# Two-tile score pipelines: 16 heads in four 32-row parts, four score banks, and pipelines that go by pairs of tiles

## The chip, the cores and the metric

The kernel runs on one core of a Trainium2 chip. The metric is the device time of one execution in microseconds (us), taken as the median of several executions. An execution that is profiled also leaves a trace, from which the busy times, the waits and the clock that TensorE was granted are read.

## The reference

`x` has 2 batches of 1024 tokens of width 256; `ctx` has 64 keys per batch. Four blocks follow one another, each a gated cross attention over the 64 keys and a gated feed-forward part:

```python
x = x + tanh(g_xattn[i]) * xattn_i(layernorm(x), ctx, ctx)
x = x + tanh(g_ffn[i]) * ffn_i(layernorm(x))
```

Two of the four attentions matter here: that of block 1 and that of block 3. Both have 16 heads of 16 channels:

```python
qh, kh, vh = heads(q @ Wq + bq), heads(k @ Wk + bk), heads(v @ Wv + bv)
score = einsum('bhqd,bhkd->bhqk', qh, kh) / sqrt(16)
score = where(kv_mask[:, None, None, :], score, -10000.0)   # block 1: one mask of the 64 keys per batch
score = where(m[:, None, :, :] == 0, -1e9, score)  # block 3: a mask for each token and key
attn = softmax(score, axis=-1)
out = einsum('bhqk,bhkd->bhqd', attn, vh) @ Wo + bo
```

The feed-forward part behind block 1's attention is dense: eight gated experts, all of them applied to every token. That behind block 3's attention routes each token to two of eight experts, which needs a router on the attention's result first.

## The kernel before

The 2048 tokens are 16 tiles of 128 (`NT`), in four groups of four (`TG`, `NG`); a group is 512 tokens wide. TensorE works in float32 here, in which one matmul of the program leaves two records in the trace (and two weight loads).

`class Heads` (L420) holds one such attention; there are two objects, `heads1` and `heads3`. `setup` (L431) makes keys and values: `kblk` is the keys in block-diagonal form, so that one matmul over the channels of several heads gives the separate scores of each head, `vblk` the same for the values. For the key mask of `heads1` it also makes `kbias` (L456), whose rows 0 and 1 hold -9984 and -16 where a key is masked and whose other rows are zero; a matmul with a matrix of ones (`ones_b`) adds both to every token. For `heads3` it makes `dropm` (L465), the mask by token and key, which a matmul with the unit matrix (`ident_b`) adds to the scores.

`pipeline` (L636) runs over the tiles one by one. In each round it calls, for different tiles, the four steps:

- `scores` (L520) takes two banks of PSUM (`ps_s`) for one tile. The mask goes in first by two matmuls of 512 columns (L536). Then four matmuls (L542), each with 64 channels (four heads) as its rows, add the scores: rows 0 to 63 into one bank, rows 64 to 127 into the other, 256 columns each. VectorE takes the maximum of each bank by head (L562) and subtracts it (L563); ScalarE takes the exponential of all 1024 columns (L572). In `heads3` the first bank (`by_head`, L429) goes another way: VectorE takes the negative maximum (L555), and ScalarE makes subtraction and exponential in one, head by head, eight instructions of 64 columns (L558); only the second bank is subtracted on VectorE, and its exponential is L570.
- `turned` (L575) transposes the result on TensorE, eight matmuls of 128 columns (L584) into two banks, which ScalarE copies to `pT` (L181).
- `quotients` (L592) makes, with matmuls of 32 columns of weights (L603), the denominators (`halves`) and the weighted values (`vblk`) of all heads in one bank. ScalarE makes the reciprocal through a logarithm (L615, L616), and VectorE multiplies and refines it (L617 to L619).
- `output` (L627) applies the last weights (L273 with `wo`) and adds the gated result to `xs` (L634).

Beside these, `between` advances two lists of generators: `ready`, which makes the norm, its transposes (L265) and the queries (`query_steps`, L505: L273 with `wq`, L511) of the group ahead, and `onward`, which makes what comes after for the group behind: in `heads1` the norm and the transposed input of the dense feed-forward part, in `heads3` the norm and the router's logits.

The order in which instructions stand on each engine is not that of the calls alone: the program is scheduled when it is built, so parts of one step may stand between parts of another. Buffers come from pools. In `middle` (L1776), which runs `heads1`, PSUM's eight banks are shared out as 4 for scores (`ps`), 2 for transposes (`pt`) and 2 for queries, quotients and outputs (`py`). In `last_attention` (L1866), which runs `heads3`, they are 3, 2 and 2, and 1 for the router (`pr`). The dense part after `heads1` (`ffn1_group`; L1676, L1374 and L1721 are matmuls of it) takes its banks when these pools end.

Of the kernel before, what the change touches and what calls it, by code (L numbers as in the profile page):

```python
# [8 lines left out]
F32 = mybir.dt.float32  # L9
# [35 lines left out]
def kernel(ctx: ExitStack, tc: tile.TileContext, a: dict, out: bass.AP):  # L45
# [372 lines left out]


    class Heads:  # L420


        def __init__(self, pre, c_bk, r_bv, r_bo, gate, key_mask, full_mask):
            self.pre, self.c_bq, self.c_bk, self.gate = pre, c_bk - 1, c_bk, gate
            self.r_bv, self.r_bo = r_bv, r_bo
            self.key_mask, self.full_mask = key_mask, full_mask
            self.live, self.qT = {}, {}

            self.by_head = 0 if full_mask is None else 1  # L429

        def setup(self, psp, tag):  # L431
# [11 lines left out]
            if key_mask is not None:  # L443
# [7 lines left out]
                two_rows = held.tile([P, 2], F32, name="two_rows")  # L451
                V.tensor_scalar(two_rows[:, 0:1], partid, 0.0, 9984.0, ALU.is_equal, ALU.mult)
                V.tensor_scalar(two_rows[:, 1:2], partid, 1.0, 16.0, ALU.is_equal, ALU.mult)
                V.tensor_add(two_rows[:, 0:1], two_rows[:, 0:1], two_rows[:, 1:2])
                self.kbias = held.tile([P, B * SK], BF16, name="kbias")
                V.tensor_scalar(self.kbias, km, -1.0, two_rows[:, 0:1], ALU.add, ALU.mult)  # L456
# [63 lines left out]
        def scores(self, tt, pools):  # L520

            b, t = tt // (NT // B), tt % TG
            two, pss = pools["two"], pools["ps"]
            pr = two.tile([P, H, SK], F32, name="pr")
            prv = pr.rearrange("p (c r j) k -> p r c j k", c=NC, r=2)
            HC = H // NC


            pair = [pss.tile([P, 512], F32, name="ps_s") for _ in range(2)]

            if self.full_mask is not None:
                whose, drop = ident_b, self.dropm[:, tt, :]
            else:
                whose, drop = ones_b, self.kbias[:, b * SK : (b + 1) * SK]
            for r in range(2):
                T.matmul(  # L536
                    pair[r], lhsT=whose, rhs=drop.unsqueeze(1).to_broadcast([P, HC, SK]),
                    start=True, stop=False, skip_group_check=True,
                )
            for c in range(NC):  # L540
                for r in range(2):
                    T.matmul(  # L542
                        pair[r][:, c * 256 : (c + 1) * 256],
                        lhsT=self.qT[tt // TG][r * 64 : (r + 1) * 64, c, t * P : (t + 1) * P],
                        rhs=self.kblk[r * 64 : (r + 1) * 64, b, c, r * 4 : (r + 1) * 4]
                        .rearrange("p j k -> p (j k)"),
                        start=False, stop=True, skip_group_check=True,
                    )
            for r in range(2):
                ps3 = pair[r].rearrange("p (j k) -> p j k", k=SK)  # L550
                ps4 = pair[r].rearrange("p (c j k) -> p c j k", c=NC, k=SK)
                mx = two.tile([P, HC], F32, name="mx")
                if r < self.by_head:

                    V.tensor_reduce(mx, ps3, AX.X, ALU.max, negate=True)  # L555
                    for j in range(HC):
                        c, k = divmod(j, HC // NC)
                        A.activation(  # L558
                            prv[:, r, c, k], ps3[:, j], AF.Exp, bias=mx[:, j : j + 1]
# [4 lines left out]
                    prv[:, r], ps4,  # L564
                    mx.rearrange("p (c j) -> p c j", c=NC).unsqueeze(3)
                    .to_broadcast([P, NC, HC // NC, SK]),
                    ALU.subtract,
                )
                if self.by_head:
                    A.activation(prv[:, r], prv[:, r], AF.Exp)  # L570
            if not self.by_head:
                A.activation(pr, pr, AF.Exp)  # L572
            self.live[tt] = pr

        def turned(self, tt, pools):  # L575
# [4 lines left out]
            for q4 in range(2):  # L580
                pst = pt.tile([P, 512], F32, name="ps_tr")
                for i in range(4):
# [3 lines left out]
                        pr[:, 2 * hp : 2 * hp + 2, :].rearrange("p a k -> p (a k)"),  # L586
# [49 lines left out]
        def pipeline(self, pools, ready, onward):  # L636
# [9 lines left out]
            for i in range(NT + 2):  # L646
                if i < NT and i % TG == 0:
                    advance(coming, 99)
                    if i + TG < NT:
                        coming.append(ready(i // TG + 1))  # L650
                if 0 <= i - 1 < NT:
                    self.turned(i - 1, pools)
                if i < NT:
                    self.scores(i, pools)
                between(2)
                if 0 <= i - 1 < NT:
                    self.quotients(i - 1, pools)
                between(2)
                if 0 <= i - 2:
                    self.output(i - 2, pools)  # L660
                if i > TG and i % TG == 1:
                    gone.append(onward(i // TG - 1))
# [1113 lines left out]
    def middle():  # L1776
        with ExitStack() as es:
# [4 lines left out]
            with ExitStack() as wide:  # L1782
                def wpl(name, bufs, **kw):
# [6 lines left out]
                    "pt": wpl("pt", 2, space=PSUM), "ps": wpl("ps", 4, space=PSUM),  # L1790
                    "py": wpl("py", 2, space=PSUM),
                }
                hp, hTp = wpl("h", 2), wpl("hT", 2)
# [20 lines left out]
            class Both:  # L1814


                @staticmethod
                def tile(shape, dtype, name):
                    return py.tile(shape, dtype, name="ps_y")

# [45 lines left out]
    def last_attention():  # L1866
        with ExitStack() as es:
            def pool(name, bufs, **kw):
# [7 lines left out]
                "two": pool("two", 3), "nq": 2, "by_log": True, "pt": pool("pt", 2, space=PSUM),  # L1876
                "ps": pool("ps", 3, space=PSUM), "py": pool("py", 2, space=PSUM),
# [129 lines left out]
```

## Time and profile before

| What | Value |
|---|---|
| Median of three executions | 2232.72 us (2231.45 to 2238.72) |
| The profiled execution | 2234.43 us |
| Its span | 2232.7 us |
| Mean granted clock of TensorE | 0.947 of full speed |
| TensorE (PE) busy | 2057.9 us, 92% of the span |
| VectorE (DVE) busy | 1333.7 us, 60% |
| ScalarE (ACT) busy | 940.6 us, 42% |
| GpSimd (POOL) busy | 1124.9 us, 50% |
| First and last score matmul (L542) | 348.4 and 2026.0 us |

The span is the time from the first to the last instruction of the profiled execution; 1.7 us of its time lie around it. PE is the matmuls, PEld the loads of weights into TensorE, which go on beside matmuls. A record's length is latency as well as work, so what a matmul occupies is read from the distance between the starts of records. In the rows of the slices each digit is a fortieth of the span, in tenths: 9 is busy for 90% or more, and the clock row shows the clock granted to TensorE. An arrow in brackets names what ended an engine's idle time before an instruction.

### The profile page before, as it was taken

The numbers are of one execution on the slowest core, as the hardware profiler recorded it, in microseconds if no ns is written. First come the engines' busy times: TensorE is split into PE (matmuls) and PEld (weight loads), VectorE is DVE, ScalarE is ACT, GpSimd is POOL, SyncE is SP. The second block draws the span as 40 slices with busy tenths as digits, with TensorE's granted clock in tenths as the row PEclk, the third lists the DMA queues.
The fourth block names the chain that finished last, engine by engine and source line by source line (L and its number), as shares of the span: only waits on it lengthen the run. The fifth ranks groups of instructions, "written<-read, shape, count | busy, mean of one in ns | idle before, by whom it ended". The sixth has DMA issues, their size and how long they took to land. (4 is left out here: it accounts for less than half of the span.)

```text
span 2232.7 us, 31616 instructions
## 1 busy us (share of the span) xinstructions
PE 2057.9 (92%) x11296; PEld 1733.4 (78%) x11296; DVE 1333.7 (60%) x3059; ACT 940.6 (42%) x2124; POOL 1124.9 (50%) x1265
## 2 busy tenths in 40 slices
PE   5659998999999999999999999999986999797897
PEld 3449985688888788888888887888864998465797
DVE  6841127856666666666666567566675566677464
ACT  4424435643333433333433333333332555473454
POOL 3226644136666456666466664666630664210673
PEclk9859998999999999999999999999985999797899
DMA  3146451012222222222222222222231444111352
GB/s 112 39 164 191 101 168 58 6 62 85 88 91 86 76 93 87 85 85 85 82 88 85 85 88 82 85 85 90 90 96 45 130 123 121 52 39 58 103 148 60
DMA packets 108533, 201.05 MB, mean 90 GB/s; under 512 B 20053, under 2 KB 47961, under 8 KB 105791
## 3 DMA queue, kind: packets, MB, share of 16 engines
q1 hardware_dynamic: 83144, 162.18, 22.7%
q0 software_dynamic: 19728, 36.03, 6.3%
q8 instruction: 90, 1.47, 0.3%
q10 hardware_dynamic: 5504, 0.82, 0.2%
q14 instruction: 67, 0.54, 0.1%
HBM read 206.89 MB, written 21.91 MB: 102 GB/s over the span
## 5 line engine op out<-in xcount | busy, mean ns | idle before, releaser
L1676 PE MATMUL ps_b<-xsum,w 128*128 128x256 f32 x1536 | 385.7, 380 | 0.1
L1307 POOL TENSOR_TENSOR w<-w 128x256 f32<-128x256 f32 x220 | 163.1, 742 | 376.3 <-DMA w<-in_L_Wu_dram 191.1
L1676 PEld LDWEIGHTS ps_b<-xsum,w 128*128 128x128 f32 x1536 | 290.7, 190 | 45.6 <-issue 4.5
L1358 ACT COPY u<-ps_b 128x512 f32<-128x512 f32 (+5 forms) x242 | 118.9, 491 | 436.0 <-PE ps_b L1721 252.6
L1676 PE MATMUL ps_a<-hT,w 128*128 128x256 f32 x1024 | 265.0, 380 | 0.2 <-ACT ps_b L1340 0.2
L1676 PEld LDWEIGHTS ps_a<-hT,w 128*128 128x128 f32 x1024 | 193.4, 190 | 27.1 <-ACT ps_b L1340 0.9
L1308 POOL TENSOR_TENSOR w<-w 128x256 f32<-128x256 f32 x220 | 192.2, 874 | 0.0
L1310 POOL TENSOR_TENSOR w<-w 128x256 f32<-128x256 f32 x220 | 183.4, 834 | 16.6
L1309 POOL TENSOR_TENSOR w<-w 128x256 f32<-128x256 f32 x220 | 190.4, 866 | 0.0
L1340 ACT COPY ps_b<-ps_a 128x512 f32<-128x512 f32 (+5 forms) x242 | 115.4, 477 | 120.4 <-DVE b L1706 68.7
L1702 DVE TENSOR_TENSOR c<-ps_e,u 128x512 f32<-128x512 f32 x64 | 44.2, 691 | 153.9 <-ACT u L1358 153.9
L1738 POOL TENSOR_TENSOR m<-m,accT 128x256 f32<-128x256 f32 x60 | 71.7, 1195 | 125.7 <-ACT m L1346 125.7
L1346 ACT COPY m<-ps_e 128x512 f32<-128x512 f32 (+5 forms) x242 | 117.9, 487 | 38.0 <-PE ps_e L1721 26.3
L1676 PE MATMUL ps_e<-hT,w 128*128 128x256 f32 x512 | 133.2, 382 | 0.0
L1676 PE MATMUL ps_e<-xsum,w 128*128 128x256 f32 x512 | 132.9, 380 | 0.0
L1721 PE MATMUL ps_b<-t,w 128*128 128x256 f32 x512 | 131.9, 382 | 0.2 <-DVE accT L1739 0.2
L1721 PE MATMUL ps_a<-b,w 128*128 128x256 f32 x512 | 131.4, 379 | 0.0
L250 POOL TENSOR_SCALAR h<-xs,rstd,off 128x256 f32<-128x256 f32 x32 | 19.9, 632 | 220.3 <-DVE off L242 121.6
L1703 DVE TENSOR_TENSOR b<-b,c 128x512 f32<-128x512 f32 x128 | 117.1, 915 | 4.3
L1683 ACT ACTIVATE b<-b 128x512 f32<-128x512 f32 x128 | 80.7, 630 | 67.1 <-DVE b L1691 62.7
L1676 PEld LDWEIGHTS ps_e<-hT,w 128*128 128x128 f32 x512 | 97.3, 191 | 14.7 <-ACT m L1346 1.2
L1721 PEld LDWEIGHTS ps_b<-t,w 128*128 128x128 f32 x512 | 97.6, 191 | 14.0 <-DVE accT L1739 0.7
(419 smaller groups left out, 4488.8 us busy)
## 6 DMA issues: line engine op xcount, KB each, us to landing
w<-in_L_Wg_dram SPq DMA_DIRECT2D x64, 512.0 KB
w<-in_L_Wu_dram SPq DMA_DIRECT2D x64, 512.0 KB
w<-in_L_Wd_dram SPq DMA_DIRECT2D x64, 512.0 KB
w<-in_L_W_dram SPq DMA_DIRECT2D x64, 512.0 KB
hd_L<-h SPq DMA_DIRECT2D x8, 512.0 KB
b<-b2d SPq DMA_DIRECT2D x23, 128.0 KB
xs<-in_x_dram SPq DMA_DIRECT2D x4, 512.0 KB
xd<-xs SPq DMA_DIRECT2D x4, 512.0 KB
```

The source lines that it names most:

```text
L1307: lambda: eng.tensor_add(s[0], a21, a22),
L1308: lambda: eng.tensor_sub(s[1], s[0], a11),
L1309: lambda: eng.tensor_sub(s[2], a11, a21),
L1310: lambda: eng.tensor_sub(s[3], a12, s[1]),
L1340: A.copy(self.b, self.pa)
L1346: A.copy(self.sb5, self.pe)
L1358: A.copy(u2, self.b)
L1676: T.matmul(ps[:, q * 256 : (q + 1) * 256], lhsT=lhs[kind][:, q, :], rhs=xr[kind], start=(first and q == 0), stop=True, skip_group_check=True,)
L1683: done[0] = A.activation(dst, src, AF.Silu)
L1703: V.tensor_mul(m[name], m[name], c)
L1721: T.matmul(ps, lhsT=wd[kind][:, q, :], rhs=m["rhs"][kind][:, q * 256 : (q + 1) * 256], start=(clear and q == 0), stop=True, skip_group_che ...
L1738: G.tensor_add(sb, sb, acc[:, i, j])
```

## The change

The change has three parts.

1. `scores` takes a pair of tiles instead of one. The 16 heads lie in four parts of 32 channels (two heads each) instead of two of 64. Part r of both tiles goes into bank r of four, with matmuls of 32 rows and 128 columns that are placed on rows 32r to 32r+31 of the array (`tile_position`): 16 matmuls a pair instead of 8. VectorE and ScalarE then work bank by bank, a bank being one part of both tiles: as many reductions, subtractions and exponentials for a pair as before. `pr` has two buffers of a pair each. `by_head` becomes 2 of 4 banks, the same share as 1 of 2.
2. The key mask of `heads1` is one row in each of the four 32-row parts (`kbias` with -100, weights `hundred` with 100), so that a pair takes four matmuls of 32 rows and 512 columns. The mask of `heads3` stays a matmul with the unit matrix over all 128 rows: eight of 256 columns for a pair, where there were four of 512.
3. `pipeline` goes over pairs: `turned` of the first tile, `scores` of the next pair, `quotients` of the first, `turned` of the second, `output` of the tile before, `quotients` of the second, `output` of the first. The pools `pt` and `py` become one: 4 banks for scores and 4 for all else in `middle`, 4 and 3 and the router's 1 in `last_attention`.

In the changed file the lines move. The masks are L554 (`heads1`) and L546 (`heads3`), the scores L566, the maxima L579 (by head) and L585, the exponential by head L581, the subtraction L586, the exponential L594, the transposes L606, the matmuls of `quotients` L625, its logarithm and exponential L637 and L638, its products L639 to L641, the addition to `xs` L656.

```diff
--- before.py
+++ after.py
@@ -416,6 +416,16 @@
                             active[k] = None
                             at[k] += 1
 
+    def one_tag(pool):
+
+
+        class Tagged:
+            @staticmethod
+            def tile(shape, dtype, name):
+                return pool.tile(shape, dtype, name="ps_y")
+
+        return Tagged
+
 
     class Heads:
 
@@ -426,7 +436,7 @@
             self.key_mask, self.full_mask = key_mask, full_mask
             self.live, self.qT = {}, {}
 
-            self.by_head = 0 if full_mask is None else 1
+            self.by_head = 0 if full_mask is None else 2
 
         def setup(self, psp, tag):
 
@@ -448,12 +458,15 @@
                 km = held.tile([P, B * SK], F32, name="km")
                 V.tensor_single_scalar(km, km_u.bitcast(U8), 0.0, ALU.not_equal)
 
-                two_rows = held.tile([P, 2], F32, name="two_rows")
-                V.tensor_scalar(two_rows[:, 0:1], partid, 0.0, 9984.0, ALU.is_equal, ALU.mult)
-                V.tensor_scalar(two_rows[:, 1:2], partid, 1.0, 16.0, ALU.is_equal, ALU.mult)
-                V.tensor_add(two_rows[:, 0:1], two_rows[:, 0:1], two_rows[:, 1:2])
                 self.kbias = held.tile([P, B * SK], BF16, name="kbias")
-                V.tensor_scalar(self.kbias, km, -1.0, two_rows[:, 0:1], ALU.add, ALU.mult)
+                V.memset(self.kbias, 0.0)
+                for r in range(4):
+                    V.tensor_scalar(
+                        self.kbias[32 * r : 32 * r + 1, :], km[32 * r : 32 * r + 1, :],
+                        -1.0, 100.0, ALU.add, ALU.mult,
+                    )
+                self.hundred = held.tile([P, P], BF16, name="hundred")
+                V.memset(self.hundred, 100.0)
             if full_mask is not None:
                 m_w = wpool.tile([P, 2048], F32, name="w")
                 m_i = m_w[:, : NT * SK].rearrange("p (t k) -> p t k", k=SK).bitcast(I32)
@@ -517,60 +530,69 @@
             xg = xs[:, g * TG : (g + 1) * TG, :]
             G.tensor_add(xg, xg, self.bo.unsqueeze(1).to_broadcast([P, TG, D]))
 
-        def scores(self, tt, pools):
-
-            b, t = tt // (NT // B), tt % TG
+        def scores(self, pp, pools):
+
+
+            b = pp // (NT // 2 // B)
             two, pss = pools["two"], pools["ps"]
-            pr = two.tile([P, H, SK], F32, name="pr")
-            prv = pr.rearrange("p (c r j) k -> p r c j k", c=NC, r=2)
-            HC = H // NC
-
-
-            pair = [pss.tile([P, 512], F32, name="ps_s") for _ in range(2)]
+
+            pr = two.tile([P, 2 * NC, 4, 2, SK], F32, name="pr", bufs=2)
+            banks = [pss.tile([P, 512], F32, name="ps_s") for _ in range(4)]
 
             if self.full_mask is not None:
-                whose, drop = ident_b, self.dropm[:, tt, :]
+                for u in range(2):
+                    drop = self.dropm[:, 2 * pp + u, :]
+                    for r in range(4):
+                        T.matmul(
+                            banks[r][:, u * 256 : (u + 1) * 256], lhsT=ident_b,
+                            rhs=drop.unsqueeze(1).to_broadcast([P, 4, SK]),
+                            start=(u == 0), stop=False, skip_group_check=True,
+                        )
             else:
-                whose, drop = ones_b, self.kbias[:, b * SK : (b + 1) * SK]
-            for r in range(2):
-                T.matmul(
-                    pair[r], lhsT=whose, rhs=drop.unsqueeze(1).to_broadcast([P, HC, SK]),
-                    start=True, stop=False, skip_group_check=True,
-                )
-            for c in range(NC):
-                for r in range(2):
+                for r in range(4):
+                    at = slice(32 * r, 32 * r + 32)
                     T.matmul(
-                        pair[r][:, c * 256 : (c + 1) * 256],
-                        lhsT=self.qT[tt // TG][r * 64 : (r + 1) * 64, c, t * P : (t + 1) * P],
-                        rhs=self.kblk[r * 64 : (r + 1) * 64, b, c, r * 4 : (r + 1) * 4]
-                        .rearrange("p j k -> p (j k)"),
-                        start=False, stop=True, skip_group_check=True,
+                        banks[r], lhsT=self.hundred[at, :],
+                        rhs=self.kbias[at, b * SK : (b + 1) * SK].unsqueeze(1)
+                        .to_broadcast([32, 8, SK]),
+                        start=True, stop=False, skip_group_check=True,
+                        tile_position=(32 * r, 0),
                     )
-            for r in range(2):
-                ps3 = pair[r].rearrange("p (j k) -> p j k", k=SK)
-                ps4 = pair[r].rearrange("p (c j k) -> p c j k", c=NC, k=SK)
-                mx = two.tile([P, HC], F32, name="mx")
+            for u in range(2):
+                t = (2 * pp + u) % TG
+                for c in range(NC):
+                    for r in range(4):
+                        at = slice(32 * r, 32 * r + 32)
+                        T.matmul(
+                            banks[r][:, (u * NC + c) * P : (u * NC + c + 1) * P],
+                            lhsT=self.qT[2 * pp // TG][at, c, t * P : (t + 1) * P],
+                            rhs=self.kblk[at, b, c, 2 * r : 2 * r + 2]
+                            .rearrange("p j k -> p (j k)"),
+                            start=False, stop=True, skip_group_check=True,
+                            tile_position=(32 * r, 0),
+                        )
+            for r in range(4):
+                ps3 = banks[r].rearrange("p (j k) -> p j k", k=SK)
+                mx = two.tile([P, 8], F32, name="mx")
                 if r < self.by_head:
 
                     V.tensor_reduce(mx, ps3, AX.X, ALU.max, negate=True)
-                    for j in range(HC):
-                        c, k = divmod(j, HC // NC)
+                    for j in range(8):
                         A.activation(
-                            prv[:, r, c, k], ps3[:, j], AF.Exp, bias=mx[:, j : j + 1]
+                            pr[:, j // 2, r, j % 2], ps3[:, j], AF.Exp, bias=mx[:, j : j + 1]
                         )
                     continue
                 V.tensor_reduce(mx, ps3, AX.X, ALU.max)
                 V.tensor_tensor(
-                    prv[:, r], ps4,
-                    mx.rearrange("p (c j) -> p c j", c=NC).unsqueeze(3)
-                    .to_broadcast([P, NC, HC // NC, SK]),
+                    pr[:, :, r], banks[r].rearrange("p (a j k) -> p a j k", j=2, k=SK),
+                    mx.rearrange("p (a j) -> p a j", j=2).unsqueeze(3)
+                    .to_broadcast([P, 2 * NC, 2, SK]),
                     ALU.subtract,
                 )
-                if self.by_head:
-                    A.activation(prv[:, r], prv[:, r], AF.Exp)
-            if not self.by_head:
-                A.activation(pr, pr, AF.Exp)
-            self.live[tt] = pr
+            for u in range(2):
+                mine = pr[:, u * NC : (u + 1) * NC, self.by_head :]
+                A.activation(mine, mine, AF.Exp)
+            self.live[2 * pp] = self.live[2 * pp + 1] = pr
 
         def turned(self, tt, pools):
 
@@ -583,7 +605,7 @@
                     hp = q4 * 4 + i
                     T.transpose(
                         pst[:, i * P : (i + 1) * P],
-                        pr[:, 2 * hp : 2 * hp + 2, :].rearrange("p a k -> p (a k)"),
+                        pr[:, tt % 2 * NC + hp // 4, hp % 4].rearrange("p a k -> p (a k)"),
                         ident,
                     )
                 evac(1, pT[:, q4 * 4 : q4 * 4 + 4, :].rearrange("p i q -> p (i q)"), pst)
@@ -643,23 +665,34 @@
                 advance(coming)
                 advance(gone, n)
 
-            for i in range(NT + 2):
-                if i < NT and i % TG == 0:
+
+            for i in range(NT // 2 + 2):
+                if i < NT // 2 and 2 * i % TG == 0:
                     advance(coming, 99)
-                    if i + TG < NT:
-                        coming.append(ready(i // TG + 1))
-                if 0 <= i - 1 < NT:
-                    self.turned(i - 1, pools)
-                if i < NT:
+                    if 2 * i + TG < NT:
+                        coming.append(ready(2 * i // TG + 1))
+                a = 2 * (i - 1)
+                valid = 0 <= a < NT
+                if valid:
+                    self.turned(a, pools)
+                if i < NT // 2:
                     self.scores(i, pools)
                 between(2)
-                if 0 <= i - 1 < NT:
-                    self.quotients(i - 1, pools)
+                if valid:
+                    self.quotients(a, pools)
                 between(2)
-                if 0 <= i - 2:
-                    self.output(i - 2, pools)
-                if i > TG and i % TG == 1:
-                    gone.append(onward(i // TG - 1))
+                if valid:
+                    self.turned(a + 1, pools)
+                if 0 <= a - 1:
+                    self.output(a - 1, pools)
+                if a > 0 and a % TG == 0:
+                    gone.append(onward(a // TG - 1))
+                between(2)
+                if valid:
+                    self.quotients(a + 1, pools)
+                between(2)
+                if valid:
+                    self.output(a, pools)
                 between(1)
             advance(gone, 99)
 
@@ -1787,9 +1820,9 @@
 
                 pools = {
                     "two": wpl("two", 3), "nq": 2, "by_log": True,
-                    "pt": wpl("pt", 2, space=PSUM), "ps": wpl("ps", 4, space=PSUM),
-                    "py": wpl("py", 2, space=PSUM),
+                    "ps": wpl("ps", 4, space=PSUM), "py": wpl("py", 4, space=PSUM),
                 }
+                pools["pt"] = one_tag(pools["py"])
                 hp, hTp = wpl("h", 2), wpl("hT", 2)
 
                 def ready(g):
@@ -1811,13 +1844,7 @@
             hTp = es.enter_context(tc.tile_pool(reuse_waits="tile", name="mi_hT", bufs=1))
             py = es.enter_context(tc.tile_pool(reuse_waits="tile", name="mi_py", bufs=2, space=PSUM))
 
-            class Both:
-
-
-                @staticmethod
-                def tile(shape, dtype, name):
-                    return py.tile(shape, dtype, name="ps_y")
-
+            Both = one_tag(py)
             pools = {"two": two, "pt": Both, "ps": Both, "py": py}
 
             def last(g):
@@ -1873,9 +1900,10 @@
             hp, hTp, hp2, rp = pool("h", 2), pool("hT", 2), pool("h2", 2), pool("r", 2)
             pr = pool("pr", 1, space=PSUM)
             pools = {
-                "two": pool("two", 3), "nq": 2, "by_log": True, "pt": pool("pt", 2, space=PSUM),
-                "ps": pool("ps", 3, space=PSUM), "py": pool("py", 2, space=PSUM),
+                "two": pool("two", 3), "nq": 2, "by_log": True,
+                "ps": pool("ps", 4, space=PSUM), "py": pool("py", 3, space=PSUM),
             }
+            pools["pt"] = one_tag(pools["py"])
             with tc.issue_after(done[0].ins):
                 A.preload_act_table_set("natural_log_exp_and_others")
             router3.open()
```

## The prediction

> **What bounds the kernel now.** I read the page's busy rows and slices first, then cut the two stretches in which the changed functions run into windows of 20 us.
>
> ```profile
> PE 2057.9 (92%) x11296; PEld 1733.4 (78%) x11296; DVE 1333.7 (60%) x3059; ACT 940.6 (42%) x2124; POOL 1124.9 (50%) x1265
> PE   5659998999999999999999999999986999797897
> PEclk9859998999999999999999999999985999797899
> ```
>
> TensorE is busy nearly throughout. The changed functions are two stretches: the pipeline of `heads1` (338 to 457 us) and that of `heads3` (1895 to 2045 us).
>
> ```profile
> core 0: us, PE busy (x) PEld busy (x) DVE busy (x) ACT busy (x) POOL busy (x), PEclk, DMA share, GB/s
> 380.00:400.00 20.00, 20.00 (x187) 13.04 (x186) 15.27 (x44) 13.69 (x29) 4.55 (x5) 1.00 0.01 3
> 400.00:420.00 20.00, 19.64 (x183) 12.86 (x182) 14.33 (x37) 13.26 (x26) 1.09 (x2) 1.00 0.05 14
> 420.00:440.00 20.00, 19.54 (x214) 13.10 (x214) 18.19 (x46) 11.07 (x22) 0.00 (x0) 1.00 0.01 2
> ...
> 1960.00:1980.00 20.00, 19.42 (x192) 13.32 (x191) 12.87 (x46) 15.53 (x48) 4.54 (x5) 1.00 0.16 54
> 1980.00:2000.00 20.00, 19.90 (x157) 12.16 (x157) 16.44 (x66) 15.13 (x47) 1.09 (x2) 1.00 0.13 45
> 2000.00:2020.00 20.00, 19.90 (x232) 14.66 (x232) 16.09 (x70) 13.07 (x42) 0.00 (x0) 1.00 0.11 37
> ```
>
> In both, TensorE leaves 0 to 0.6 of 20 us open at full clock, so a microsecond less of its work is worth up to a microsecond. Behind it VectorE has 13 to 18 of 20 us filled and ScalarE 11 to 15.5: the room is a fifth to a third.
>
> The tile view of the scores and the timeline of TensorE give durations and order.
>
> ```profile
> L542 PE MATMUL ps_s<-kblk,qT x256: 376/376/792, 348.5 to 2026.4; 64*128 64x256 f32 x128
> L558 ACT ACTIVATE pr<-ps_s,mx x128: 296/330/407, 1926.1 to 2034.5; 128x64 f32<-128x64 f32 x128
> L562 DVE TENSOR_REDUCE mx<-ps_s x48: 655/681/692, 353.4 to 2027.1; 128x8 f32<-128x512 f32 x48
> ```
>
> ```profile
> 352.11 2.93 PE L542 MATMUL ps_s<-kblk,qT 64*128 64x256 f32 x12 [2.96 <-ACT qT L511]
> ...
> 394.80 0.59 PE L536 MATMUL ps_s<-kbias,ones_b 128*128 128x512 bf16 x2
> 395.32 1.13 PE L542 MATMUL ps_s<-kblk,qT 64*128 64x256 f32 x8
> 396.38 0.65 PE L603 MATMUL ps_y<-pT,halves 128*32 128x128 f32 x16
> 396.85 0.62 PE L603 MATMUL ps_y<-pT,vblk 128*32 128x128 f32 x16
> 397.39 1.13 PE L273 MATMUL ps_y<-wo,oT 128*128 128x256 f32 x4
> ...
> 448.74 1.04 PE L584 MATMUL ps_tr<-ident,pr 128*128 128x128 f32 x8
> 458.76 1.08 PE L265 MATMUL ps_tr<-ident,h 128*128 128x128 f32 x6 [1.32 <-POOL h L250]
> ```
>
> A float32 matmul leaves two records, and a record's length holds its latency, so I take the distance of starts: masks 0.53 us a tile (394.80 to 395.32), scores 1.06, the 32 records of L603 1.01. Within the scores the single records start in twos, 6 to 7 ns apart, each two 0.213 us after the last: 4 x 0.213 = 0.85, which leaves 0.2 us for going into and out of the 64-row tiling. L603's records start in fours, 7 ns apart, one such round each 0.109 us.
>
> **The change, part by part** (counts from the order of TensorE's instructions in the changed program).
>
> *Key masks of `heads1`.* 32 matmuls of 512 columns, 0.265 us each with their share of the wait (8.5 us; 0.216 is the column time), become 8 sets of four 32-row matmuls which, side by side, cost 0.216 + 0.05 each: 2.1 us. I count the column time alone, 6.9 - 2.1 = -4.8 us. In `heads3` 32 of 512 columns become 64 of 256: no saving in columns; at most -1.4 by 0.88 a pair for 1.06. I take 0.
>
> *Scores.* Per pair of tiles 8 x 0.213 = 1.7 us becomes, if four 32-row tiles run abreast, 8 x 0.109 = 0.87. No row shows a 32-row tile. The nearest are L542 (two row tiles abreast) and L603 (four column tiles abreast, 128 columns), and I take L603's 0.109. The Trainium skill speaks a little against it: "TensorE: Matmul & The Clock Gate", Measured speedup, has four row tiles at 3.07 times one, not 4; worked from L603's row that would be an estimated 32 x 0.109 / 3.07 = 1.14 us a pair, so 0.27 x 16 pairs = 4.3 us of the gain lost. The scheduler also cuts the 16 matmuls of a pair into pieces, between which other work stands: `heads1` has 22 pieces and 43 rounds of 0.218 (32 if uncut) for some 25 pieces and 40 rounds of 0.426 before: 9.4 for 17.0 us and three entries of 0.2 less, -8.2. `heads3` has 30 pieces and 48 rounds: 10.5 for about 15.5, with some 8 entries more (+1.6): -3.4. That each entry costs is measured (the 0.2 us above), and the skill's "TensorEngine Tiling (Array Packing)", Key Properties, says the same of changing the mode: the cut pairs of `heads3` are where the tiling pays least.
>
> TensorE's work thus falls by 13.0 us in `heads1` and 3.4 in `heads3`. VectorE and ScalarE keep their work: as many 128x512 reductions, subtractions and exponentials. What changes is when.
>
> *Filling the pipeline.* Before, the first transposes (L584 at 357.2) need one tile's four VectorE passes. Now L606 of tile 0 needs the pair's exponential, which needs eight passes of 0.60 us spacing, 4.8 us, behind all 16 score matmuls. From the queries' end I get 359.4: +2.2. In `heads3` some +1.5.
>
> *One set of score banks.* Four banks hold one pair, so a pair's masks (L554, L546) wait for the subtractions (L586) of the pair before: bank 3 comes free 4.8 us after the scores end. Before, a tile took two of four banks (three in `heads3`). TensorE has about 4.2 us of other work placed there (L606, L625, L273), so about 0.6 us stays, and the next L625 waits for pT copies on ScalarE queued behind the pair's exponentials (2 x 0.62 to 1.06): about 1 us a pair, 8 us, less the 2.5 us of such waits that `heads1` has now: +5.5. Bounds: 0 if other work always fits, and 8 x 2.2 = 18 if the masks find none of the last half of the block covered. Behind a waiting mask in TensorE's order stand the transposes and queries that feed ScalarE.
>
> *`heads3` by head.* The first two of four banks go head by head: 16 exponentials. Eight take 1.76 us in the timeline, so 3.5 us, plus two halves of 0.62: a block of 4.8 us on ScalarE in which pT, the logarithms L637/L638 and qT wait, where now it is 2.4 us (1.76 + 0.67) a tile. PSUM for transposes and outputs shrinks from four banks to three. Extra wait between 0 and 2.4 us a pair; ScalarE is filled to three quarters here, so I take 0.9: 8 x 0.9 = +7.
>
> *End of `heads1`.* The dense part's banks now include those of the joined pool, used until the last norm's transposes; these (L265, eight records) now stand ahead of the first down-projection matmuls. The 1.32 us wait at 458.76 grows to about 3.6 by my placing: +2.3. The trace shows what follows a long pause: after the 2.96 us of waiting before 352.11 the granted clock is half for 3.41 us (0.79 over the window of 340 to 360); after 1.32 us here it stayed full. One such step costs up to half of 3.41: +1.7. The lowest bound of this part is 0.
>
> *Handovers.* Each pair has some four more crossings that nothing hides (L554, L606, L625, L273 after another engine); which my placing took as free; by an estimate of 0.06 us each, half of the smallest wait of 0.15 us that the timeline of VectorE names there, 16 x 4 x 0.06 = +4, from 0 to 8. The waits above hold a part of it, so +2.
>
> *Set-up.* Memsets and one-row operations (L461 to L469) replace as many small ones, 0.2 to 0.4 us each, on VectorE long before the stretch. Nothing; 1 us if that cover were gone. The queues of SP and POOL keep their order.
>
> Sum: `heads1` -13.0 + 2.2 + 5.5 + 2.3 + 1.7 = -1.3; `heads3` -3.4 + 1.5 + 7 = +5.1; handovers +2: +5.8 on 2234.4 (span 2232.7 and 1.7 around it) gives 2240.2. The profiled run is itself 1.7 us above the median of the runs shown, so against the median I get 2238.5 to 2240 and write 2240.
>
> **Rivals.** About 0.3%, 6.7 us, is what a measurement of this kernel can tell from no change.
>
> 1. *Coupling* (0.45): as summed. For it: VectorE's block of 4.8 us and ScalarE's 15.5 of 20 us. 2236 to 2254, nine tenths above +0.3%.
> 2. *Waits and savings cancel* (0.20): the stalls of `heads3` are near 0.3 us a pair rather than 0.9, no clock step: 2234.4 + 5.8 - 4.8 - 1.7 = 2233.
> 3. *TensorE stays the bound, faster* (0.25): the windows that show 20.00 of 20 us speak for it. The saving -16.4 is kept, with fills +3.7 and end +2.3 and a stall of at most 0.2 us a pair (+3.2) less 2.5 of waits that go: -9.7, about 2224, or 2217 without fill and end. It decides where the stalls and handovers of a pair are under 0.5 us.
> 4. *Row tiles do not run abreast* (0.10): 32 x 0.109 = 3.5 us a pair for 2.1 now, 16 x 1.4 = +22, masks of `heads1` saving nothing: about 2256. Two abreast instead of four is a milder form: scores save nothing, 2242 to 2246.
>
> So faster 0.25 (rival 3), within 0.3% 0.25 (rival 2 and a tenth of the first), slower 0.50. The range 2218 to 2257 leaves out the best of rival 3 and the worst of 1 and 4; the likeliest case alone is 2236 to 2254.
>
> **What would show it.** L566 records starting in fours, rounds of 0.109 us; if in ones or twos, rival 4. TensorE's idle time ahead of L554 and L546 released by L586, ahead of L625 by L181; if the sum in 360 to 440 us is under 4 us, rival 3. The end of `heads1`: an idle stretch over 3 us before L265 and a clock under 1.00 just after. In `heads3`: L581 in blocks of 3.5 us and idle TensorE behind them. The start of the dense part and the end of `heads3`, set against before, give the share of each. It is wrong if the dense part starts over 5 us earlier.

## The result, and the profile after

The changed kernel takes 2260.8 us (median of four, 2251.77 to 2267.5) against 2234.26 us before (median of four too): 1.0102 times as long, interval 1.0075 to 1.0129, so some 23 us slower (17 to 29). The profiled execution took 2255.67 us, 21 us more than that of before. The sign was forecast; the size was 6 us, and 2260.8 lies outside the range of 2218 to 2257.

The page of the changed kernel, the same rows as before: TensorE has almost the same busy time, for less work, as will be seen; a fortieth of the span is too coarse a slice to show where.

```profile
PE 2055.9 (91%) x11584; PEld 1747.2 (78%) x11584; DVE 1334.8 (59%) x3061; ACT 941.0 (42%) x2124; POOL 1121.7 (50%) x1265
PE   6659998899999999999999999999986999796797
PEclk9869998999999999999999999999985999897899
```

The windows of the two stretches tell more (the columns are as before; the clock is the third number from the right).

```profile
380.00:400.00 20.00, 17.84 (x150) 12.47 (x150) 12.42 (x38) 11.72 (x25) 2.16 (x4) 0.83 0.01 3
400.00:420.00 20.00, 17.20 (x199) 12.16 (x198) 17.48 (x37) 9.98 (x19) 2.63 (x1) 0.91 0.00 1
420.00:440.00 20.00, 17.69 (x210) 13.26 (x208) 15.79 (x43) 12.69 (x24) 1.09 (x2) 0.95 0.06 15
440.00:460.00 20.00, 16.19 (x198) 12.26 (x196) 12.45 (x35) 11.18 (x23) 1.09 (x2) 0.88 0.00 1
...
1980.00:2000.00 20.00, 17.36 (x179) 13.88 (x180) 10.96 (x38) 13.18 (x41) 3.19 (x5) 0.83 0.15 54
```

Where TensorE left 0 to 0.5 us open at a clock of 1.00, it now leaves 2 to 4 open, and its clock is 0.83 to 0.95. The timeline of TensorE shows one such place:

```profile
376.74 0.66 PE L265 MATMUL ps_y<-ident,h 128*128 128x128 f32 x4
377.33 0.39 PE L554 MATMUL ps_s<-kbias,hundred 32*128 32x512 bf16 x2
378.55 0.37 PE L554 MATMUL ps_s<-kbias,hundred 32*128 32x512 bf16 x1 [0.83 <-DVE pr L586]
379.15 0.37 PE L554 MATMUL ps_s<-kbias,hundred 32*128 32x512 bf16 x1 [0.23 <-DVE pr L586]
379.15 0.71 PE L566 MATMUL ps_s<-kblk,qT 32*128 32x128 f32 x12
380.87 2.07 PE L273 MATMUL ps_y<-wo,oT 128*128 128x256 f32 x4 [1.00 <-DVE oT L641]
382.74 1.06 PE L265 MATMUL ps_y<-ident,h 128*128 128x128 f32 x4
383.59 1.91 PE L606 MATMUL ps_y<-ident,pr 128*128 128x128 f32 x8
```

The masks of the next pair wait for the last banks of the pair before; once the scores are in, the output's matmul waits for L641, whose turn on VectorE comes behind the block of score passes. Then the clock goes to half from 380.1 to 386.9 us: the four matmuls of `wo` at 380.87 last 2.07 us where they took 1.13 before, the eight transposes 1.91 where they took 1.09.

The waits of TensorE from 340 to 480 us, the longest rows:

```profile
PE ps_y L265 <- POOL h L250: 7.3, 4, 3.5
PE ps_s L554 <- DVE pr L586: 4.4, 7, 1.4
PE ps_y L273 <- DVE oT L641: 3.9, 4, 1.0
```

The counterparts of the first two before, from 340 to 460 us (L536 is the mask, L563 the subtraction; no wait for L641's counterpart, L619, is in its list):

```profile
PE ps_tr L265 <- POOL h L250: 2.5, 3, 1.3
PE ps_s L536 <- DVE pr L563: 0.3, 1, 0.3
```

To sum a stretch up I take it from the first query matmul of `heads1` to the 120th matmul of the dense part, and split it into time without a matmul or weight load (idle), the loss by half clock (half of the busy time that lies in half-clock stretches), and the rest, TensorE's work at full clock. This work is the length of records and so holds latency.

| | to last score | from there | total | idle | loss by half clock | work |
|---|---|---|---|---|---|---|
| before | 99.8 | 44.4 | 144.2 | 7.5 | 2.2 | 134.4 |
| change | 99.2 | 61.2 | 160.5 | 21.1 | 16.2 | 123.2 |

The work did fall, by 11.2 us. Idle time rose by 13.6, and half clock took another 14.0: +16.3. For `heads3`, from its first score to the 20th matmul of the experts behind it, the same split (work, half clock, idle; rounded) gives 160.0 us = 116.8 + 16.6 + 26.5 before and 167.4 = 111.0 + 18.6 + 37.7 with the change: less work by 5.8, 11.2 more idle, 1.9 more by the clock: +7.4. Each profile is one execution: where the code of a stretch is the same, it repeated within 2 us in `heads1` and within 5 in `heads3` in the profiles below.

### The profile page after: what moved, and what is told of

Read it like the earlier page. It is cut to its first block, busy times and chain, and to the rows that moved or that the text cites. A ratio compares the mean times of both kernels' runs of the same rounds, so it can differ in the third digit from the quotient of the medians.

```text
span 2253.6 us, 32177 instructions
## 1 busy us (share of the span) xinstructions
PE 2055.9 (91%) x11584; PEld 1747.2 (78%) x11584; DVE 1334.8 (59%) x3061; ACT 941.0 (42%) x2124; POOL 1121.7 (50%) x1265
## 5 line engine op out<-in xcount | busy, mean ns | idle before, releaser
L1343 POOL TENSOR_TENSOR w<-w 128x256 f32<-128x256 f32 x220 | 183.2, 833 | 16.6
L250 POOL TENSOR_SCALAR h<-xs,rstd,off 128x256 f32<-128x256 f32 x32 | 18.2, 579 | 230.7 <-DVE off L242 138.1
L1709 PEld LDWEIGHTS ps_e<-hT,w 128*128 128x128 f32 x512 | 97.2, 191 | 15.9 <-ACT m L1379 2.9
L1709 PEld LDWEIGHTS ps_e<-xsum,w 128*128 128x128 f32 x512 | 97.1, 191 | 15.2 <-issue 1.8
```

Of the source, the lines that this page charges most:

```text
L1343: lambda: eng.tensor_sub(s[3], a12, s[1]),
L1709: T.matmul(ps[:, q * 256 : (q + 1) * 256], lhsT=lhs[kind][:, q, :], rhs=xr[kind], start=(first and q == 0), stop=True, skip_group_check=True,)
```

## The experiments

Three theories stood. W: the pairing makes TensorE wait, and what is taken from TensorE is only waited away. R or T: the row tiling itself is dear. B: TensorE bounds, as the windows of before suggest. All ratios are to the kernel before on the same chip.

**e1, the key mask alone**, in the kernel before:

```diff
-whose, drop = ones_b, self.kbias[:, b * SK : (b + 1) * SK]
+at, n = slice(64 * r, 64 * r + 64), 64
+whose, drop = self.hundred, self.kbias[:, b * SK : (b + 1) * SK]
...
-    pair[r], lhsT=whose, rhs=drop.unsqueeze(1).to_broadcast([P, HC, SK]),
+    pair[r], lhsT=whose[at, :],
+    rhs=drop[at].unsqueeze(1).to_broadcast([n, HC, SK]),
```

> The kernel before, with one thing of the change alone: the key mask of heads1 by one row in each of two 64-row parts, two matmuls side by side for a tile instead of two one after the other. Tiles stay single, pools stay. Theory W (the loss is waits of TensorE that the pairing of tiles makes, and half-clock steps that follow them): nothing here makes a wait, TensorE bounds the stretch, so 16 x 0.216 = 3.5 us less work, and up to 16 x 0.1 more where mask and scores share a tiling mode: 2.5 to 5 us faster than before. Theory R (32- and 64-row tiling costs more than it saves): no gain, 0 to 3 us slower.

1.0002 (0.999 to 1.0014): no gain, or 2 us at most. In the profile the work of the first stretch fell from 134.4 to 130.0 us, idle rose from 7.5 to 10.5, and the stretch took 143.2 us for 144.2. Two rows of its waits show where it went; the first stood at 1.0 us, three times, before:

```profile
PE ps_tr L589 <- ACT pr L577: 3.3, 4, 1.0
PE ps_y L273 <- DVE oT L624: 1.5, 1, 1.5
```

Transposes now wait for the exponentials. The kernel before was thus hardly bound by TensorE alone: a stretch whose windows show 98 to 100% busy had almost nothing to give for 4.4 us less work. That speaks against B, and it is what the prediction's first step got wrong.

**e2 and e3, the change in one stretch only** (the other class and its pools as before).

> The whole change in heads1 only; heads3 and its pools as before. The profiles put the end of the dense part 13.4 us later with the change, the rest of the 21 us behind it. Theory W: the two stretches are independent, so +12 to +15 us. Theory H (heads3, where sixteen exponentials by head stand in a row on ScalarE and the banks are one fewer, carries the loss, and the first stretch's delay is made up in the rest): +2 to +6 us.

> The whole change in heads3 only; heads1 and its pools as before. Theory W: what e2 leaves, +5 to +9 us. Theory H: +15 us or more.

1.0071 (1.0051 to 1.0092), some 16 us, and 1.0053 (1.0033 to 1.0073), some 12 us. Both lose; which loses more the intervals (11 to 21 us and 7 to 16) do not tell. Their sum, 1.0124, agrees with the change within the intervals. H's 2 to 6 us for e2 falls; W's 5 to 9 us for `heads3` lies at the low end of e3's interval.

**e4, pairs without 32-row tiling**: each bank holds one half of the heads of one tile, and the masks are those of before.

```diff
+pair = banks[2 * u : 2 * u + 2]
...
-    banks[r][:, (u * NC + c) * P : (u * NC + c + 1) * P],
-    lhsT=self.qT[2 * pp // TG][at, c, t * P : (t + 1) * P],
+    pair[r][:, c * 256 : (c + 1) * 256],
+    lhsT=self.qT[tt // TG][r * 64 : (r + 1) * 64, c, t * P : (t + 1) * P],
```

> The change without its tiling: pairs of tiles, four banks, joined pools and the order by pairs stay, but the scores are the 64-row matmuls of 256 columns of before, each bank holding one half of the heads of one tile, and the masks are the full-row ones of before. TensorE has about 13 us more work in heads1 than in the changed kernel, and a bank pair is complete after half of the matmuls. Theory W (the pairing makes the waits): as slow as the change or slower, +15 to +30 us over before, with half-clock steps in both stretches. Theory R (the tiling is what costs): the pairing alone is near before, -3 to +6 us.

1.0036 (1.0023 to 1.005), some 8 us: between the two theories. Its `heads3` takes 159.6 us, as before (160.0), with the pools of the change there; the half that goes head by head is one bank of each tile, so that eight exponentials stand together and not sixteen. It has 8.4 us more work in the first stretch than the change and is still 9.0 us shorter there (151.5), with a loss by half clock of 4.5 instead of 16.2 us.

**e5, the tiling undone but the banks kept**: 64-row matmuls into banks that still hold one part of both tiles.

```diff
-for r in range(4):
-    at = slice(32 * r, 32 * r + 32)
+for r in (0, 2, 1, 3):
+    at = slice(64 * (r // 2), 64 * (r // 2) + 64)
...
-        tile_position=(32 * r, 0),
```

> The changed kernel with its four banks, each holding one part of the heads of both tiles, its masks, its pools and its order by pairs, but each score matmul takes 64 rows instead of 32 (the 32 more of the block-diagonal keys add zeros), so two run abreast instead of four: about 16 x 0.87 = 14 us more work for TensorE in the two stretches together. Theory B (TensorE bounds): 10 to 14 us slower than the change, about 2272 to 2276. Theory W (the pairing's order and banks make the waits, and the time saved on TensorE is only waited away): within 4 us of the change, 20 us over before. Theory T (the 32-row tiling itself is dear, by its mode changes or by a lower clock under it): near the pairs with whole-tile banks, 6 to 12 us over before.

1.0073 (1.0046 to 1.01), against the change between 15 us faster and 2 slower; its two stretches take 160.0 and 167.3 us, as the change's 160.5 and 167.4. More work, measured at 7.6 us in the first stretch (130.8 for 123.2), costs nothing there: it stands where waits were (idle 15.8 for 21.1) and where the clock was half (13.4 lost for 16.2). B falls. T has no support in the stretches, but the medians leave it room for some us. Between e4 and e5 the matmuls have the same rows; what differs is the banks, and with them the width of a score matmul, the key mask's form and the sixteen exponentials in a row. That costs some 8 us (2 to 15). The likely reason is the layout: four banks that all wait for all 16 score matmuls and come free over VectorE's whole block, where two banks of a tile come free after half of it.

**e6, more work in the changed kernel**: every denominator twice.

```diff
-for at, den in ((D, True), (0, False)):
+for at, den in ((D, True), (D, True), (0, False)):
```

> The changed kernel with the denominators' matmuls of every tile issued twice (the second overwrites the same values): 16 more records a tile, four abreast, 0.44 us, so 14 us more work for TensorE over the two stretches; the scheduler places other instructions somewhat differently around it. Theory B (TensorE bounds): 14 us slower than the change. Theory W: the work falls mostly into waits: 0 to 6 us slower. Theory C (the loss is mainly half clock, which waits bring about, and more work in their place keeps the clock up): as fast as the change or up to 6 us faster, with fewer half-clock steps in 350 to 470 us than the 35 us there are now.

1.0091 (1.0056 to 1.0126), by its time as slow as the change. In its profile the stretches take 162.2 and 175.3 us, 9.6 more than the change's (8 of them in `heads3`), so that the profile and the medians don't agree on whether it is free; half clock in the first stretch is 32.6 us for 34.8. That more work would keep the clock up (C) is not seen, and this run decides no more than that.

**e7 and e8, no maxima**, in the changed kernel and in that before: a constant zero is subtracted.

```diff
-mx = two.tile([P, 8], F32, name="mx")
+mx = zeros[:, :8]
...
-V.tensor_reduce(mx, ps3, AX.X, ALU.max)
```

> The changed kernel without the maxima of the scores in both pipelines (a constant zero is subtracted instead): VectorE's block for a pair falls from eight passes of 0.60 us to four (three in heads3, where half of the banks have no subtraction). Theory W with VectorE's block as its cause: the waits for L586 and L641 go, and with them half-clock steps: 10 to 18 us faster than the change, at or below before. If the waits come from elsewhere (ScalarE's queue, the drain at the end of each stretch): 0 to 6 us faster.

> The control for it: the kernel before without the maxima of the scores. VectorE loses 32 x 4 x 0.60 / 2 = 38 us of busy time in the two stretches. If TensorE bounds the kernel before: 0 to 3 us faster. If VectorE's share sets the pace of it too: 6 us or more faster.

e7 is at 0.9989 (0.9967 to 1.001), some 25 us faster than the change (18 to 33); e8 at 0.9971 (0.9958 to 0.9984). Without the maxima the change costs 0.2% (-0.1 to 0.4) instead of 1.0%. So the loss hangs on VectorE's block, more strongly than any theory had it; since the maxima also stand between scores and exponentials, shorter block and shorter chain are not told apart.

By the profile it is not the sum of the waits that goes. The first stretch takes 147.4 us for the change's 160.5, with as much idle time (21.3 for 21.1). The waits for L586 are gone, those for the output's products and for L250 are not (L640 is L641 here):

```profile
PE ps_y L265 <- POOL h L250: 12.0, 5, 3.5
PE ps_y L273 <- DVE oT L640: 2.8, 3, 1.4
```

What goes is half clock (6.8 us lost for 16.2) and 3.9 us in the length of the same records. In e8 VectorE is busy 1305.2 us for 1333.7, and the kernel is 6 us faster (4 to 9); its profile has the gain in `heads3` (152.8 us for 160.0) and none in `heads1` (147.4 for 144.2). By this profile VectorE matters to `heads3` of the kernel before; what bounds its `heads1` neither e1 nor e8 shows.

A window of e7 shows waits that are spread: 2.9 to 3.5 us open in 20, and the clock still up.

```profile
380.00:400.00 20.00, 17.09 (x224) 12.20 (x225) 11.61 (x34) 12.95 (x29) 4.52 (x5) 1.00 0.01 3
400.00:420.00 20.00, 16.50 (x204) 10.77 (x202) 13.45 (x36) 12.10 (x24) 0.29 (x1) 1.00 0.05 15
```

**e9 and e10, the pools of `heads1` as before**, in the change and in e4.

```diff
-"ps": wpl("ps", 4, space=PSUM), "py": wpl("py", 4, space=PSUM),
+"pt": wpl("pt", 2, space=PSUM), "ps": wpl("ps", 4, space=PSUM),
+"py": wpl("py", 2, space=PSUM),
...
-pools["pt"] = one_tag(pools["py"])
```

The end of `heads1` in the changed kernel is why:

```profile
445.86 1.99 PE L1709 MATMUL ps_a<-hT,w 128*128 128x256 f32 x8 [0.41 <-DVE pr L586]
450.85 0.33 PE L265 MATMUL ps_y<-ident,h 128*128 128x128 f32 x1 [2.99 <-POOL h L250]
...
466.83 1.97 PE L265 MATMUL ps_y<-ident,h 128*128 128x128 f32 x8 [3.47 <-POOL h L250]
468.60 3.62 PE L1407 MATMUL ps_b<-rows,ident 128*128 128x512 f32 x4
472.01 1.16 PE L1709 MATMUL ps_e<-xsum,w 128*128 128x256 f32 x4
```

Only `ps_a` of the dense part starts early; `ps_b` and `ps_e` stand behind the last norm's transposes. Before, matmuls into `ps_e` filled the drain from 448.31 us on.

> The changed kernel with the pools of heads1 as before: two banks for transposes, four for scores, two for the rest, instead of four and a joined four; heads3 unchanged. Where the dense part's banks come from is then as before. In the profile of the change the stretch from the last score of heads1 to the dense part's 120th matmul is 61.2 us for 44.4 before. Theory P (the joined pool holds the dense part's banks to the end of the drain, so that its matmuls cannot fill it): 8 to 14 us of the 16.8 come back. Theory D (the drain is long because the last two tiles are done as a pair, whatever the banks): 0 to 3 us come back.

> The pairs with 64-row scores and whole-tile banks (0.36% over before), with the pools of heads1 as before. Its stretch to the last score is 92.9 us for 99.8 before, its drain 58.6 for 44.4. Theory P: the drain falls to 44 to 50 us, and the kernel is level with before or up to 6 us faster. Theory D: it stays where it was, 6 to 10 us over before.

e9: 1.0044 (1.0025 to 1.0064), some 13 us less than the change (6 to 20). Its first stretch is 150.2 us for 160.5; idle 16.5 for 21.1, loss by half clock 8.9 for 16.2. About half of these 10.3 us lies in the drain (56.0 for 61.2), as theory P has it, though less than its 8 to 14; the other half lies ahead of the last score (94.3 for 99.2), which it did not foresee. That transposes, quotients, queries and outputs had to take turns in one ring of four may be its cause; no run tells it from the scheduler's other order. e10: 1.0001 (0.9988 to 1.0014), level with before; its first stretch takes 144.7 us. The windows of e10 have the clock back:

```profile
390.00:410.00 20.00, 18.72 (x171) 10.91 (x172) 15.14 (x43) 11.39 (x25) 2.18 (x4) 1.00 0.01 2
410.00:430.00 20.00, 18.97 (x195) 12.25 (x185) 15.27 (x36) 12.01 (x24) 2.37 (x1) 1.00 0.06 15
```

The drain stays 8.2 us longer than before (52.6), and the scores end 7.7 us sooner: the pairs by themselves shift work to the end and win nothing. The whole time is what P foresaw, the drain lies between P and D.

Change, e4, e9 and e10 are the four ways to join two layouts with two pools of `heads1`. The layout by parts (with its tiling and, in `heads3`, its sixteen exponentials in a row) costs 15 us with the joined pool (change against e4; 8 to 22) and 10 with the pools of before (e9 against e10; 4 to 15). The joined pool costs 13 us with the layout by parts (6 to 20) and 8 with whole-tile banks (e4 against e10; 4 to 12). By either path the sum is the 23 us of the change.

**e11, the block issued in two halves**, with the first tile's quotients between them.

> The changed kernel with VectorE's block of a pair cut in two where it is issued: the passes over banks 0 and 1, then those of the first tile's quotients, then banks 2 and 3. The same instructions, in another order on VectorE. Theory W with the block as cause of the waits for L641 (3.9 us, four times 1.0) and of the half clock behind them: 4 to 8 us faster than the change. Theory S (banks 2 and 3 come free later, so the wait of the masks L554 grows by as much): within 3 us of the change.

1.0104 (1.0079 to 1.0128), as the change: theory S by the times. Its profile took 2248.7 us, far below its own median of 2261.9, and has a first stretch of 154.8 us, with more idle (23.0) and less half clock (8.7 lost) than the change. L554's waits did not grow there, as S has it, but shrank to 1.7 us, while those for the output's product (L641's counterpart) went up to 5.0; so S's reason is not met. Half clock varies between executions also where the code is the same (`heads3` as before lost 16.6 us to it in the kernel before, 21.1 in e1 and 21.2 in e2), and one profile does not show the split's worth.

**e12, e10 with the key mask of e1.**

> The kernel that came out level with before (pairs of tiles, 64-row scores in whole-tile banks, the pools of heads1 as before), with the key mask of heads1 by one row in each of two 64-row parts added: 16 x 0.216 = 3.5 us less for TensorE. Theory W (TensorE is not what bounds these stretches any more; work taken from it is waited away): within 2 us of the kernel without it, level with before. Theory B: 3 to 5 us faster than before, the best version.

0.9991 (0.9973 to 1.0009): nothing to be told from before. No version here that keeps the maxima is shown to beat the kernel before.

## Why the prediction was wrong

Set against its sum: the two stretches grew by 23.7 us (16.3 and 7.4) where +5.8 was said. Half clock took 15.9 us for the 1.7 of the sum, waits 24.8 for 20.5 (fills, banks, `heads3`, end and handovers together), and work fell by 17.0 for 16.4. So the step that failed is the clock: 14 of the 18 us that are missing. That the saving agrees so well is in part luck, since 13.0 and 3.4 were said for the two stretches and 11.2 and 5.8 measured.

- *"A microsecond less of its work is worth up to a microsecond"*: it was worth next to none. In e1 taking work away, in the stretches of e5 adding it, moved next to nothing. The prediction itself says that a record's length holds latency, and yet reads 20.00 of 20 us as full. Column time tells more: each record counted at the spacing of starts (0.216 us for 256 float32 columns, or 512 of bf16), times the share of the array's rows and columns that it takes, so that tiles abreast count once. From 360 to 440 us of the kernel before, matmul records cover 97.5% of the time, and column time is 64.0 of the 80 us. On the other side VectorE's 18.19 of 20 us left a tenth, not a fifth.
- *Four row tiles abreast*: right. In the uncut 30 records at 371.74 us they start in fours, 6 to 7 ns apart, a round each 0.112 us for most. Single full-array records of 128 columns (L584 at 448.74 us before) start 0.109 apart, so four in 0.112 are 3.9 times as fast as one after another. The 3.07 of the Trainium skill ("TensorE: Matmul & The Clock Gate", Measured speedup), given there for 512 columns, is not seen at 128. Rival 4 is out.
- *One set of score banks, +5.5*: the right waits (L554 for L586, 4.4 us in seven, longest 1.4), with 1.7 us for L625 behind pT: 6.1 us for the 8 worked out. Beside it stand L641's 3.9 us, queued behind the block on VectorE, which the working did not have.
- *The clock, +1.7 once*: the term that failed most in `heads1`. It is 14.0 us more than before: 34.8 us at half clock for 4.8. I had priced one step at the end and none for the pairs, because the long pause of 2.96 us was followed by one and 1.32 us by none. Waits of 0.83, 0.23 and 1.00 us together brought a step of 6.8 us (the timeline above). In `heads3` the clock took 1.9 us more, where none was priced.
- *End of `heads1`, +2.3*: the place was right and the wait of 3.6 us was met (3.47), but another of 2.99 us stands ahead of it, before 450.85; both were followed by half clock, and the joined pool kept the dense part's matmuls from filling them: in e9 the wait of L265 for L250 falls from 7.3 to 0.2 us. e9 gives the pool in all about 13 us.
- *`heads3`, +5.1*: +7.4 in its stretch by the profile, +12 (7 to 16) by e3. The block of sixteen exponentials was seen, 3.38 us at 2037.44 for the 3.5 worked out, and behind it a pT copy for which TensorE waits 1.82 us. With whole-tile banks and the same pools of 4, 3 and 1 the stretch takes 159.6 and 158.7 us (e4, e10), so layout and block carry this loss and the smaller pool does not. Where the rest of e3's loss lies is not settled.

So the likeliest case had the mechanism (coupling outweighs the saving) and mis-sized two terms: the clock behind short waits, and the joined pool. By the experiments the layout by parts costs 10 us and the pool 13, or 15 and 8 in the other order. How much of the layout's share is its 32-row tiling is open (e5 leaves it between nothing and 15 us), and every edit also moves other instructions in the program's schedule, which no run holds fixed.

## What to carry to other kernels

Before pricing saved TensorE work, find out whether it bounds: count column time and not busy records, take passes from another engine, or put redundant matmuls in, and see whether the time follows. Here the tiled parts of a pair went to separate banks; these come free one after another as VectorE reads them, and by the experiments that costs more than the faster matmuls bring. A wait on TensorE costs its length and, where waits gather, half clock besides: as much again in `heads1` (13.6 and 14.0 us), a sixth in `heads3` (11.2 and 1.9). And a joined buffer pool can hold back the stage that comes next.

## What of the hardware was not expected

The clock does not need a long pause to fall. I cut the time from 376 us on into the 3.41 us steps in which the clock changes, and took for each the time without TensorE work. In the changed kernel half clock follows each step with 2.28 us or more (2.32, 2.47, 2.28) and two of 1.29 and 1.30 us; one of 1.31 and all of 0.93 and less left a full clock full. In e5 1.65 us brought it down, in e7 1.52 did not. So waits add up: 0.83, 0.23 and 1.00 us between 377.7 and 380.9 stand ahead of and in 6.8 us of half clock.

But idle time gives no clean border. A step of the changed kernel at 352.8 fell with 0.87 us, and steps of 1.66 to 1.99 us in e9 and e11 did not. Column time gives a better one. In the 14 traces, from 335 to 480 and from 1920 to 2060 us, 953 steps had a full clock. All 76 with up to 1.00 us of column time were followed by half clock, none with over 1.41 us was, and of the 67 between 28 were. The best border in each of the two stretches sorts 5 steps wrongly by column time and 35 by idle time. The step at 352.8 holds 0.76 us. The masks and scores of a pair add up to 2.6 us of column time before and to 1.1 with the change, so a step that holds little else lies near the border: an estimate from the spacings above. By this reading the saved work itself leaves the clock less to stand on. No run tests it, and e6's added matmuls did not keep the clock up.

The Trainium skill ("TensorE: Matmul & The Clock Gate", What's actually happening) has the clock fall after an idle window of about 3.4 us; the traces agree on the window and not on its having to be wholly idle.
